# Gate and hid of a feed-forward layer by seven half products in a fixed plan of two slots

## The chip, the cores and the metric

The kernel runs on one core of one Trainium2 chip. The metric is the device time of one launch in microseconds (us). Short names of the engines: PE is TensorE (matmuls), DVE is VectorE, ACT is ScalarE, POOL is GpSimd, SP is the engine that issues most of the DMAs.

## The reference

One transformer block in float32 on `x` of 4 x 1024 x 512 (4 sequences, 1024 tokens, 512 features), with 16 heads of 32 features and a hidden width of 2048. Both norms take a scale and an offset from a condition vector `t`.

```python
def _tc_rmsnorm(x, t, gw, gb, bw, bb):
    g = (t @ gw.T + gb)[:, None, :]
    b = (t @ bw.T + bb)[:, None, :]
    inv_rms = jax.lax.rsqrt(jnp.mean(x * x, axis=-1, keepdims=True) + EPS)
    return g * x * inv_rms + b

def _swiglu(x, gate_w, hid_w, out_w):
    return jax.nn.silu(x @ gate_w.T) * (x @ hid_w.T) @ out_w.T

y = x + _attention(_tc_rmsnorm(x, t, g1w, g1b, b1w, b1b), Wq, Wk, Wv, Wo)
y = y + _swiglu(_tc_rmsnorm(y, t, g2w, g2b, b2w, b2b), gate_w, hid_w, out_w)
out = x + y
```

The change concerns the two products `x @ gate_w.T` and `x @ hid_w.T`.

## The kernel before

Features lie on the 128 partitions in four pieces (`C` = 4), tokens along the free dimension in eight blocks of 512 (`NBLK` = 8, `NB` = 512). The order on PE, DVE, ACT and POOL is the order in which the program is written; SP's DMAs are issued in their order too, each as soon as its buffer is free.

The work runs in *slots*, one turn of the loop `while g < NR + 10`. A slot takes one unit of attention: four heads, 256 queries, two key tiles of 128. Four slots make a group (four heads, 256 queries, all 1024 keys); `kind = g % 4` tells where in the group a slot stands. There are 256 such slots, 32 for each token block. In slot `g` PE computes the scores of unit `g` (`scores`, line 263) into the four PSUM banks of `ps_sc`, and ACT copies them to SBUF (`keep`, 270). DVE keeps a running maximum over the group (`running_max`, 278 and 280, and `fold_max`, 284). In the next slot of kind 0 PE transposes the maxima (`max_T`, mt, 290), DVE reduces them and splits them into three bfloat16 parts (`parts`, 296 to 301), and PE transposes those (`parts_T`, pt, 306), to be copied by ACT (mT, 308). In the slot of kind 1, `spread` (sp, 317) multiplies them out to all partitions and ACT copies the result to `shift` (318). Five slots after its scores a unit is shifted (`shifted`, DVE, 322) and exponentiated (`exponential`, ACT, 327), and a slot later weighted with the values (`weighted`, av, PE, 337). POOL adds the exponentiated tiles of a group with accumulating DMAs (`accumulate`, 351) and folds their two halves with one more (`fold_sum`, 359); `sums` (369) adds over partitions on PE in the slot of kind 3.

Between these pieces stand *chains*: four matmuls of 128 x 128 by 128 x 512 that sum into one bank of the pool `ps` (three banks), and one eviction. Each matmul of a chain is written as four strips of 32 output rows (`mm`, line 102), since `columns` is 32 for most of the loop; the hardware's records show two for each float32 matmul. Chains are key, query and value projections (`project_kq`, `project_v`), the output projection (`project_out`, po), gate and hid (`hidden`, ph: for each token block and each of 16 feature blocks `f`, one chain for gate, one for hid, over four input pieces) and the contraction with `out_w` (`contract`, pc: for four feature blocks together, one chain for each of the four output pieces). They wait in one queue; each slot adds `PACE` = 1.6 to a credit, and each chain taken costs one. Gate is evicted by a tanh on ACT (450) and one DVE operation (452), hid by one DVE operation (454), a contraction by one (466). What is left when attention ends, the feed-forward of the last token block and part of the one before, runs in a tail with nothing beside it.

Weights of a feature block are loaded by `load_f` (512 KB of gate and hid, 256 KB of `out_w`). Norms of the token blocks are put at fixed slots with `between` and `after`.

Of the kernel before, what the change touches and what calls it, by code (L numbers as in the profile page):

```python
# [24 lines left out]
def tile_cond_transformer_block(  # L25
# [7 lines left out]
    vo_w: bass.AP,  # L33
# [19 lines left out]
    PACE = 1.6  # L53
# [6 lines left out]
    ps = ctx.enter_context(tc.tile_pool(name="ps", bufs=3, space=PSUM))  # L60
# [34 lines left out]


    columns = [P]

    def mm(dst, w, moving, start: bool, stop: bool):
        n = columns[0]  # L100
        for k in range(0, P, n):
            nc.tensor.matmul(dst[k : k + n, :], w[:, k : k + n], moving, start=start, stop=stop)  # L102
# [3 lines left out]
    x2, res, h, fw, ow = {}, {}, {}, {}, {}  # L106
    state = {}

    def norm_squares(dst, tag: str, k: int):

        sq = [sb.tile([P, NB], F32, tag="t", name=f"sq{tag}_{2 * k + i}", bufs=3) for i in range(2)]
# [63 lines left out]
    def norm_sum(dst, tag: str):  # L175

        pm = ps.tile([P, NB], F32, tag="w", name=f"pm{tag}")
        for c in range(C):
            sq = sb.tile([P, NB], F32, tag="t", name=f"sq{tag}_{c}", bufs=3)
            nc.scalar.activation(sq, dst[:, c, :], AF.Square)  # L180
            nc.tensor.matmul(pm, ones_mean, sq, start=(c == 0), stop=(c == C - 1))
# [21 lines left out]
    def load_wkq(hg: int):  # L203
        t = sb.tile([P, 2, C, P], F32, tag="fw", name=f"wkq{hg}", bufs=3)
# [4 lines left out]
    def project_kq(b: int, hg: int, which: int, half: int):  # L209
        pp = ps.tile([P, NB], F32, tag="w", name=f"pkq{b}_{hg}_{which}_{half}")  # L210
# [14 lines left out]
    def project_v(b: int, kt: int):  # L225
        half, col = divmod(kt * P, NB)
        pp = ps.tile([P, NB], F32, tag="w", name=f"pv{b}_{kt}")
# [24 lines left out]
    def scores(r: int):  # L252
# [13 lines left out]
        raw[r] = sb.tile([P, HG, 2, HQ], F32, tag="raw", name=f"raw{r}", bufs=RAW)  # L266
        state["sc", r] = sc

    def keep(r: int):
        nc.scalar.copy(raw[r], state.pop(("sc", r)))  # L270

    def running_max(r: int):
        j, u = divmod(r, UN)
        if u == 0:
            return
        if u == 1:
            rmax[j] = sb.tile([P, HG, 2, HQ], F32, tag="rmax", name=f"rmax{j}")
            nc.vector.tensor_tensor(rmax[j], raw[r - 1], raw[r], ALU.max)  # L278
        else:
            nc.vector.tensor_tensor(rmax[j], rmax[j], raw[r], ALU.max)  # L280

    def fold_max(j: int):
        t = rmax[j]
        nc.vector.tensor_tensor(t[:, :, 0, :], t[:, :, 0, :], t[:, :, 1, :], ALU.max)

    def max_T(j: int):
        pt = ps_sc.tile([P, HQ // P, HG, P], F32, tag="sc", name=f"mt{j}")
        for qt in range(HQ // P):
            for i in range(HG):
                nc.tensor.transpose(pt[:, qt, i, :], rmax[j][:, i, 0, qt * P : (qt + 1) * P], ident)  # L290
# [19 lines left out]
    def spread(j: int):  # L310

        shift[j] = sb.tile([P, HG, HQ], F32, tag="shift", name=f"shift{j}")
        t = mT.pop(j)
        for k in range(0, HG, 2):
# [458 lines left out]
```

## Time and profile before

| what | us |
|---|---|
| median of three runs | 2572.88 (2571.51 to 2577.04) |
| the profiled execution | 2572.48 |
| its span | 2570.7 |
| first and last start of a score matmul | 49.3, 2207.0 |
| PE busy in the loop's stretch 565 to 2265 | 1654.21 of 1700 |
| DVE, ACT busy in the same stretch | 1187.01, 941.97 |
| PE busy in the tail, 2265 to 2571 | 298.27 of 306 |

The granted TensorE clock is 0.988 in the mean. Busy time is the union of an engine's instructions; [...]records overlap, and a chain's price is best read from start to start. DMA is the mean busy share of the 16 engines: 0.86 in the stretch of the loop, 0.22 in the tail. 242.24 MB of 475.76 MB go through POOL's queue, which takes 50.8% of the engines' time.

### The profile page before, as it was taken

To read this page: it belongs to the slowest core of one execution; us is meant where nothing else is said; L and a number is where in the kernel's file an instruction comes from. 1 tells how busy PE (TensorE), PEld (TensorE's weight loads), DVE (VectorE), ACT (ScalarE), POOL (GpSimd) and SP (SyncE) were. 2 spreads that over 40 slices of the span, in tenths; PEclk is the share of its full clock that TensorE was granted. 3 is DMA by queue.
4 is the path that set the end of the run, shared out by engine and by line. 5 is a ranking of instruction groups with operands and counts; after the bars stand their busy time and mean duration, and the time that the engine had idled before them with its cause. 6 is when DMAs were issued, how large, how long until landed. Compare 5 with 4: busy or idle time off the path is not lost.

```text
span 2570.7 us, 51245 instructions
## 1 busy us (share of the span) xinstructions
PE 2480.6 (96%) x22520; PEld 1014.6 (39%) x22520; DVE 1595.7 (62%) x1508; ACT 1330.2 (52%) x1229; POOL 256.6 (10%) x271
## 2 busy tenths in 40 slices
PE   8999998999999999999999999999999999999999
PEld 3333333333343443434333343334344434334444
DVE  2666766567777766667777676766777777632221
ACT  3676776565565555555565555555665566410000
POOL 0011111111111111111111111111111111100000
PEclk9999999999999999999999999999999999999999
DMA  5699998898897988888888788888898898922221
GB/s 190 191 250 230 234 232 185 197 229 191 189 200 176 215 194 200 185 214 191 186 193 214 171 194 192 194 204 184 196 205 212 192 207 187 205 77 82 83 82 52
DMA packets 187644, 475.76 MB, mean 185 GB/s; under 512 B 37407, under 2 KB 95767, under 8 KB 159134
## 3 DMA queue, kind: packets, MB, share of 16 engines
q0 software_dynamic: 62448, 242.24, 50.8%
q1 hardware_dynamic: 91392, 219.45, 25.2%
q10 hardware_dynamic: 33582, 10.80, 1.9%
q8 instruction: 177, 2.90, 0.4%
q14 instruction: 45, 0.37, 0.0%
HBM read 196.10 MB, written 34.09 MB: 90 GB/s over the span
## 4 chain that ended last, share of the span: by engine, by line
PE 56%; DMA 9%; DVE 6%; ACT 4%; issue 3%; ACTq 2%; POOL 0%; DVEq 0%; POOLq 0%
PE ph L102 24%; PE pc L102 14%; DMA raw<-raw 7%; PE sc L263 6%; PE av L337 5%; PE po L102 3%; DVE raw L322 3%; ACTq L153 2%; ACT raw L327 2%; PE mt L290 1%; ACT raw L270 1%; PE sum L369 1%; DVE top L296 1%; PE sp L317 1%; DMA res<-x 1%
## 5 line engine op out<-in xcount | busy, mean ns | idle before, releaser
L102 PE MATMUL ph<-x,fw 128*32 128x512 f32 (+1 forms) x6056 | 921.2, 597 | 2.9 <-ACT x L167 2.2
L322 DVE TENSOR_TENSOR raw<-raw,shift 128x2048 f32<-128x2048 f32 x256 | 582.0, 2274 | 109.6 <-ACT shift L318 109.3
L270 ACT COPY raw<-sc 128x2048 f32<-128x2048 f32 x256 | 478.9, 1871 | 306.6 <-PE sc L263 214.4
L327 ACT ACTIVATE raw<-raw 128x2048 f32<-128x2048 f32 x256 | 489.9, 1914 | 129.7 <-DVE raw L322 129.4
L102 PEld LDWEIGHTS ph<-x,fw 128*32 128x32 f32 (+1 forms) x6056 | 309.2, 121 | 501.5 <-issue 472.0
L102 PE MATMUL pc<-h,ow 128*32 128x512 f32 (+1 forms) x3112 | 460.4, 597 | 2.0 <-DVE h L454 2.0
L280 DVE TENSOR_TENSOR rmax<-rmax,raw 128x2048 f32<-128x2048 f32 x128 | 293.0, 2289 | 125.4 <-ACT raw L270 125.3
L351 POOL DMA_DIRECT2D raw<-raw x192 | 169.0, 880 | 1499.0 <-DMA raw<-raw 713.2
L263 PE MATMUL sc<-kq 32*128 32x256 f32 x4096 | 295.1, 402 | 7.5 <-ACT raw L270 7.5
L337 PE MATMUL av<-raw,v 128*32 128x256 f32 x4096 | 279.8, 392 | 14.6 <-ACT avs L363 11.0
L452 DVE SCALAR_TENSOR_TENSOR h<-t,ph 128x512 f32<-128x512 f32 x128 | 88.0, 688 | 299.5 <-ACT t L450 299.5
L263 PEld LDWEIGHTS sc<-kq 32*128 32x128 f32 x4096 | 186.0, 185 | 171.0 <-issue 120.9
L102 PEld LDWEIGHTS pc<-h,ow 128*32 128x32 f32 (+1 forms) x3112 | 152.1, 119 | 254.8 <-issue 235.1
L102 PE MATMUL pkq<-y,wkq 128*32 128x512 f32 (+1 forms) x1784 | 234.8, 599 | 5.9 <-ACT y L167 4.1
L450 ACT ACTIVATE t<-ph 128x512 f32<-128x512 f32 x128 | 76.0, 593 | 313.2 <-PE ph L102 277.4
L466 DVE SCALAR_TENSOR_TENSOR res<-pc,res 128x512 f32<-128x512 f32 x128 | 88.1, 689 | 153.0 <-PE pc L102 152.8
L337 PEld LDWEIGHTS av<-raw,v 128*32 128x32 f32 x4096 | 108.8, 110 | 141.7 <-issue 49.1
L278 DVE TENSOR_TENSOR rmax<-raw,raw 128x2048 f32<-128x2048 f32 x64 | 146.2, 2284 | 24.4 <-ACT raw L270 24.4
L454 DVE TENSOR_TENSOR h<-ph,h 128x512 f32<-128x512 f32 x128 | 87.9, 687 | 86.0 <-PE ph L102 85.8
L308 ACT COPY mT<-pt 12x256 bf16<-12x256 bf16 x64 | 23.1, 360 | 214.5 <-PE pt L306 175.9
L359 POOL DMA_DIRECT2D raw<-raw x64 | 82.9, 1296 | 505.4 <-DMA raw<-raw 462.3
L102 PEld LDWEIGHTS pkq<-y,wkq 128*32 128x32 f32 (+1 forms) x1784 | 72.1, 116 | 136.0 <-issue 121.4
(81 smaller groups left out, 1299.8 us busy)
## 6 DMA issues: line engine op xcount, KB each, us to landing
raw<-raw POOLq DMA_DIRECT2D x192, 1024.0 KB, 8.6
fw<-in_gh_w SPq DMA_DIRECT2D x128, 512.0 KB
ow<-in_out_w SPq DMA_DIRECT2D x128, 256.0 KB
raw<-raw POOLq DMA_DIRECT2D x64, 512.0 KB, 6.4
wkq<-in_kq_w SPq DMA_DIRECT2D x32, 512.0 KB
v<-vs SPq DMA_DIRECT2D x32, 512.0 KB
kq<-kqs SPq DMA_DIRECT2D x31, 512.0 KB
kqs<-st SPq DMA_DIRECT2D x61, 256.0 KB
```

Of the source, the lines that this page charges most:

```text
L102: nc.tensor.matmul(dst[k : k + n, :], w[:, k : k + n], moving, start=start, stop=stop)
L263: nc.tensor.matmul(sc[:, i, k, :], t[rows, kt * P : (kt + 1) * P], t[rows, q0 : q0 + HQ], start=True, stop=True)
L270: nc.scalar.copy(raw[r], state.pop(("sc", r)))
L278: nc.vector.tensor_tensor(rmax[j], raw[r - 1], raw[r], ALU.max)
L280: nc.vector.tensor_tensor(rmax[j], rmax[j], raw[r], ALU.max)
L322: nc.vector.tensor_tensor(t, t, shift[r // UN].unsqueeze(2).to_broadcast([P, HG, 2, HQ]), ALU.add)
L327: nc.scalar.activation(raw[r], raw[r], AF.Exp)
L337: nc.tensor.matmul(av[j][i * DH : (i + 1) * DH, :], v[m][:, kt, i * DH : (i + 1) * DH], raw[r][:, i, k, :], start=(kt == 0), stop=(kt == K ...
L351: nc.gpsimd.dma_start(out=acc[j].rearrange("p h k q -> p (h k q)"), in_=raw[r].rearrange("p h k q -> p (h k q)"), accum_op=ALU.add,)
L452: nc.vector.scalar_tensor_tensor(h[n, f], t, 1.0, pp, ALU.add, ALU.mult)
L454: nc.vector.tensor_tensor(h[n, f], pp, h[n, f], ALU.mult)
L466: nc.vector.scalar_tensor_tensor(r, pp, 0.5, r, ALU.mult, ALU.add)
```

## The change

A feature block's gate and hid are treated as one product of a 2 x 2 block matrix (gate over hid; input pieces 0 and 1, 2 and 3) with a 2 x 2 block of the tokens (the same pieces; 256 tokens left, 256 right), and computed by Strassen's seven products in place of eight. Each product is two matmuls of 128 x 128 by 128 x 256, again in strips of 32 rows.

- `weight_sums` builds four sums of the weights once for each feature block, on DVE, in slots 4 to 51, and stores them in DRAM (`s_w`); `token_sums` builds four differences of the tokens once for each token block, on DVE, one of them in place.
- The products are named 1 to 7. Bank A (`bank_a`, of `ps`) holds gate: product 1 on its left and 5 on its right (`pair_15`). ACT copies product 5 to SBUF (`take_5`), DVE writes left + product 5 to the right (`add_15`), then products 2 and 6 are added by PE onto what stands there (`pair_26`), and product 3 onto the right (`pair_3`). Bank B (`bank_b`, the one bank of `ps_b`) holds hid: ACT copies the right half of A to its right half (`copy_156`) before product 3 comes, PE adds product 7 (`pair_7`), DVE writes right minus product 5 to its left (`sub_5`), and PE adds product 4 (`pair_4`). Then gate and hid are evicted as before (`gate_tanh`, `gate`, `hidden`).
- `ps` has two banks, not three; the third is `ps_b`. Before the token sums exist, `bank` gives every third chain of a projection to `ps_b`.
- From slot `FS` = 60 on, two slots take one feature block, numbered `p` over all token blocks, in a written order: the even slot has `pair_26` and one contraction (`filler`, number `p` - 4; for the first four `p`, a projection kept back for that), the odd slot `pair_7`, `pair_3`, `pair_15` of the next block and `pair_4`. Output projections come in odd slots where they are due. Before that slot the queue runs with `PACE` = 1.5. The tail takes `p` from 104 on.
- `raw` is laid out by key tile first, the running maximum is two DVE operations of 1024 elements a slot (one in the first of a group), and the fold at the end is gone. The fold of the row sums (`fold_sum`) is a DVE operation at the head of the slot of kind 3, not a DMA. `spread` is split in two halves, one ahead of the scores and one behind. The norms of a token block move by a slot here and there.
- `load_f` has two parts, 512 KB and 384 KB; `out_w` and `Wo` are laid out so that each contraction and each output projection loads its own 256 KB.

```diff
-    PACE = 1.6
+    PACE = 1.5
...
-    ps = ctx.enter_context(tc.tile_pool(name="ps", bufs=3, space=PSUM))
+    ps = ctx.enter_context(tc.tile_pool(name="ps", bufs=2, space=PSUM))
+    ps_b = ctx.enter_context(tc.tile_pool(name="ps_b", bufs=1, space=PSUM))
...
+    def bank(name: str):
+
+        turn[0] += 1
+        if "sums" not in state and turn[0] % 3 == 0:
+            return ps_b.tile([P, NB], F32, tag="wb", name=name)
+        return ps.tile([P, NB], F32, tag="w", name=name)
...
-        raw[r] = sb.tile([P, HG, 2, HQ], F32, tag="raw", name=f"raw{r}", bufs=RAW)
+        raw[r] = sb.tile([P, 2, HG, HQ], F32, tag="raw", name=f"raw{r}", bufs=RAW)
...
+    def running_max(r: int, k: int):
         j, u = divmod(r, UN)
+        if u:
+            nc.vector.tensor_tensor(rmax[j], rmax[j], raw[r][:, k, :, :], ALU.max)
+        elif k:
+            rmax[j] = sb.tile([P, HG, HQ], F32, tag="rmax", name=f"rmax{j}")
+            nc.vector.tensor_tensor(rmax[j], raw[r][:, 0, :, :], raw[r][:, 1, :, :], ALU.max)
...
+    def spread(j: int, k: int):
+        if k == 0:
+            shift[j] = sb.tile([P, HG, HQ], F32, tag="shift", name=f"shift{j}")
+        pp = ps.tile([P, 2, HQ], F32, tag="w", name=f"sp{j}_{k}")
+        for i in range(2):
+            nc.tensor.matmul(pp[:, i, :], select[:, k + i, :], mT[j], start=True, stop=True)
+        nc.scalar.copy(shift[j][:, k : k + 2, :], pp)
...
     def fold_sum(j: int):
         t = acc[j]
-        nc.gpsimd.dma_start(out=t[:, :, 0, :], in_=t[:, :, 1, :], accum_op=ALU.add)
+        nc.vector.tensor_tensor(t[:, 0, :, :], t[:, 0, :, :], t[:, 1, :, :], ALU.add)
...
+    def weight_sums(f: int, step: int):
+        if step == 0:
+            state["gh", f] = sb.tile([P, 2, C, P], F32, tag="fw", name=f"gh{f}", bufs=4)
+            nc.sync.dma_start(out=state["gh", f], in_=gh_w[f])
+        else:
+            t = state.pop(("gh", f))
+            a11, a12, a21, a22 = (t[:, i, k : k + 2, :] for i in range(2) for k in (0, 2))
+            o = sb.tile([P, 4, 2, P], F32, tag="fw", name=f"s{f}", bufs=4)
+            nc.vector.tensor_tensor(o[:, 0], a21, a22, ALU.add)
+            nc.vector.tensor_tensor(o[:, 1], o[:, 0], a11, ALU.subtract)
+            nc.vector.tensor_tensor(o[:, 2], a11, a21, ALU.subtract)
+            nc.vector.tensor_tensor(o[:, 3], a12, o[:, 1], ALU.subtract)
+            nc.sync.dma_start(out=s_w[f], in_=o)
...
+    def token_sums(n: int, i: int):
+        b11, b12, b21, b22 = tokens(n)
+        if "sums" not in state:
+            state["sums"] = sb.tile([P, 4, 2, HQ], F32, tag="a", name="sums", bufs=3)
+        t = state["sums"]
+        if i == 0:
+            nc.vector.tensor_tensor(t[:, 0], b12, b11, ALU.subtract)
+        elif i == 1:
+            nc.vector.tensor_tensor(t[:, 1], b22, t[:, 0], ALU.subtract)
+        elif i == 2:
+            nc.vector.tensor_tensor(b12, b22, b12, ALU.subtract)
+        else:
+            nc.vector.tensor_tensor(t[:, 2], b21, t[:, 1], ALU.subtract)
+    def load_f(p: int, part: int):
+        f = p % NF
+        fw[p, part] = sb.tile([P, 4, 2, P], F32, tag="fw", name=f"fw{p}_{part}", bufs=4)
+        if part == 0:
+            nc.sync.dma_start(out=fw[p, 0][:, 0:2], in_=gh_w[f][:, 0].rearrange("p (a c) o -> p a c o", a=2))
+            nc.sync.dma_start(out=fw[p, 0][:, 2:4], in_=s_w[f][:, 0:2])
+        else:
+            nc.sync.dma_start(out=fw[p, 1][:, 0:2], in_=s_w[f][:, 2:4])
+            nc.sync.dma_start(out=fw[p, 1][:, 2], in_=gh_w[f][:, 1, 2:4])
+    def product(dst, w, moving, start: bool = False):
+        for k in range(2):
+            mm(dst, w[:, k, :], moving[:, k, :], start and k == 0, k == 1, True)
+    LEFT, RIGHT = slice(0, HQ), slice(HQ, NB)
+    def pair_15(p: int):
+        b11 = tokens(p // NF)[0]
+        a = bank_a[p] = ps.tile([P, NB], F32, tag="w", name=f"pa{p}")
+        product(a[:, LEFT], fw[p, 0][:, 0], b11, True)
+        product(a[:, RIGHT], fw[p, 0][:, 2], state["sums"][:, 0])
+    def take_5(p: int):
+        fifth[p] = sb.tile([P, HQ], F32, tag="st", name=f"p5_{p}", bufs=2)
+        nc.scalar.copy(fifth[p], bank_a[p][:, RIGHT])
+    def add_15(p: int):
+        a = bank_a[p]
+        nc.vector.tensor_tensor(a[:, RIGHT], a[:, LEFT], fifth[p], ALU.add)
+    def pair_26(p: int):
+        a = bank_a[p]
+        product(a[:, LEFT], fw[p, 0][:, 1], tokens(p // NF)[2])
+        product(a[:, RIGHT], fw[p, 0][:, 3], state["sums"][:, 1])
+    def copy_156(p: int):
+        if "b" not in state:
+            state["b"] = ps_b.tile([P, NB], F32, tag="wb", name="pb")
+            nc.tensor.matmul(
+                state["b"], select[:, 0, :], select.rearrange("p h c -> p (h c)"), start=True, stop=True
+            )
+        bank_b[p] = state["b"]
+        nc.scalar.copy(bank_b[p][:, RIGHT], bank_a[p][:, RIGHT])
+    def pair_7(p: int):
+        product(bank_b[p][:, RIGHT], fw[p, 1][:, 0], tokens(p // NF)[1])
+    def sub_5(p: int):
+        b = bank_b[p]
+        nc.vector.tensor_tensor(b[:, LEFT], b[:, RIGHT], fifth.pop(p), ALU.subtract)
+    def pair_3(p: int):
+        product(bank_a[p][:, RIGHT], fw[p, 1][:, 1], tokens(p // NF)[3])
+    def pair_4(p: int):
+        product(bank_b[p][:, LEFT], fw[p, 1][:, 2], state["sums"][:, 2])
+    def gate_tanh(p: int):
+        state["t", p] = sb.tile([P, NB], F32, tag="t", name=f"t{p}", bufs=2)
+        nc.scalar.activation(state["t", p], bank_a[p], AF.Tanh, scale=0.5)
+    def gate(p: int):
+        h[p] = sb.tile([P, NB], F32, tag="h", name=f"h{p}", bufs=7)
+        nc.vector.scalar_tensor_tensor(h[p], state.pop(("t", p)), 1.0, bank_a.pop(p), ALU.add, ALU.mult)
+    def hidden(p: int):
+        nc.vector.tensor_tensor(h[p], bank_b.pop(p), h[p], ALU.mult)
+    def load_ow(q: int):
+        ow[q] = sb.tile([P, FG, P], F32, tag="ow", name=f"ow{q}", bufs=4)
+        nc.sync.dma_start(out=ow[q], in_=out_w[q // C % (NF // FG), q % C])
+    def contract(q: int, pp, passes):
+        for k in passes:
+            mm(pp, ow[q][:, k, :], h[q // C * FG + k], k == 0, k == FG - 1)
+    def take_contract(q: int, pp):
+        n, d = q // NF, q % C
+        r = res[n][:, d, :]
+        nc.vector.scalar_tensor_tensor(r, pp, 0.5, r, ALU.mult, ALU.add)
+        if q // C % (NF // FG) == NF // FG - 1:
+            nc.sync.dma_start(out=out[n][:, d, :], in_=r)
...
+    FS = BS + 28
+    for f in range(NF):
+        after(3 * f + 4, weight_sums, f, 0)
+        after(3 * f + 6, weight_sums, f, 1)
...
+            for i in range(3):
+                after(g0 + 26, token_sums, n, i)
+            between(g0 + 27, token_sums, n, 3)
...
+            if kind == 1 and m_on:
+                spread(j_m, 0)
             if g < NR:
                 scores(g)
-            if x_on and kind in (2, 3):
+            if kind == 1 and m_on:
+                spread(j_m, 2)
+                mT.pop(j_m)
+            if kind == 3 and s_on:
+                fold_sum(j_s)
...
+                if g == FS - 1:
+                    columns[0] = DH
+                    pair_15(0)
+                    take_5(0)
+                    add_15(0)
...
+            elif even:
+                load_f(p + 1, 1)
+                pair_26(p)
+                copy_156(p)
+                if x_on:
+                    exponential(r_x)
+                if kind == 0 and m_on:
+                    max_T(j_m)
+                    parts(j_m)
+                one, two, evict = filler(p)
+                one()
+                two()
+                if g < NR:
+                    running_max(g, 0)
+                    running_max(g, 1)
+                if evict is not None:
+                    evict()
+                for fn, a in halfway.pop(g, []):
+                    fn(*a)
+            else:
+                load_f(p + 2, 0)
+                if due or len(queue) > FG:
+                    chain(g)()
+                pair_7(p)
+                sub_5(p)
+                pair_3(p)
+                gate_tanh(p)
+                if x_on:
+                    exponential(r_x)
+                pair_15(p + 1)
+                take_5(p + 1)
+                if g < NR:
+                    running_max(g, 0)
+                gate(p)
+                if g < NR:
+                    running_max(g, 1)
+                add_15(p + 1)
+                pair_4(p)
+                hidden(p)
+                if due:
+                    chain(g)()
+                if kind == 3 and s_on:
+                    sums(j_s)
+                    if j_s < direct:
+                        sums_out(j_s)
...
+        p0 = (END - FS) // 2
+        for p in range(p0, NP_):
+            if p + 1 < NP_:
+                load_f(p + 1, 1)
+            pair_26(p)
+            copy_156(p)
+            if p == n * NF - 1:
+                token_sums(n, 0)
+                token_sums(n, 1)
+                token_sums(n, 2)
+            one, two, evict = filler(p, True)
+            one()
+            if p + 2 < NP_:
+                load_f(p + 2, 0)
+            pair_7(p)
+            sub_5(p)
+            pair_3(p)
+            gate_tanh(p)
+            gate(p)
+            if p + 1 < NP_:
+                pair_15(p + 1)
+                take_5(p + 1)
+                add_15(p + 1)
+            pair_4(p)
+            hidden(p)
+            if p == n * NF - 1:
+                token_sums(n, 3)
+            two()
+            evict()
```

## The prediction

> **What bounds the kernel now.** I read the page first, then the chain of waits in order of time over one stretch of the middle, then the timeline of a place where TensorE (PE) stands still, then single rows.
>
> ```profile
> PE 2480.6 (96%) x22520; PEld 1014.6 (39%) x22520; DVE 1595.7 (62%) x1508; ACT 1330.2 (52%) x1229; POOL 256.6 (10%) x271
> L102 PE MATMUL ph<-x,fw 128*32 128x512 f32 (+1 forms) x6056 | 921.2, 597 | 2.9 <-ACT x L167 2.2
> ```
>
> PE is busy 96% of the span, and the largest group, gate and hid (ph), stands idle for only 2.9 us in all: PE sets the time, and what leaves PE leaves the time unless a new wait takes its place. VectorE's (DVE) 62% is a mean: in the attention loop (565 to 2265 us) it is 1187.0 of 1700 us, 70%. The chain over four slots of that loop gives the price of every PE piece from start to start:
>
> ```profile
> 871.15 3.43 PE ph L102 x32
> 874.58 1.02 PE mt L290 x8
> 875.61 3.44 PE pc L102 x8
> 879.04 0.11 PE pt L306 x2
> 879.15 1.08 PE sc L263 x16
> 880.23 0.42 PE sp L317 x4
> 880.65 1.00 PE av L337 x16
> 881.65 3.43 PE pc L102 x32
> ...
> 899.57 0.43 PE sum L369 x8
> ```
>
> Scores (sc) and weighted values (av) cost 2.08 a slot, a chain of 512 columns 3.43, and a block's four extra pieces 1.02 + 0.11 + 0.42 + 0.43 = 1.98. The pieces join without a hole.
>
> ```profile
> 1015.20 0.28 PE L306 MATMUL pt<-ident_bf,split 128*128 128x128 bf16 x2
> 1015.52 0.36 ACT L308 COPY mT<-pt 12x256 bf16<-12x256 bf16 x1 [3.94 <-PE pt L306]
> 1018.17 2.28 DVE L322 TENSOR_TENSOR raw<-raw,shift 128x2048 f32<-128x2048 f32 x1
> 1019.69 1.15 PE L263 MATMUL sc<-kq 32*128 32x256 f32 x16 [1.71 <-ACT raw L270]
> 1020.37 2.28 DVE L278 TENSOR_TENSOR rmax<-raw,raw 128x2048 f32<-128x2048 f32 x1
> 1022.71 1.93 PE L337 MATMUL av<-raw,v 128*32 128x256 f32 x16 [1.87 <-ACT avs L363]
> 1024.41 5.74 PE L102 MATMUL pc<-h,ow 128*32 128x512 f32 x32
> 1030.23 0.69 DVE L466 SCALAR_TENSOR_TENSOR res<-pc,res 128x512 f32<-128x512 f32 x1 [0.78 <-PE pc L102]
> ```
>
> Three things are to be seen here. A tile that PE finishes reaches the next engine 0.05 to 0.1 us after the record's end. DVE operations back to back start 0.08 us before the record ahead ends (2.20 between two of 2.28). And after holes of 1.71 and 1.87 us close together, PE runs at half rate: 1.93 for 1.07, 5.74 for 3.62, so 3.0 us lost; after the first hole alone it still ran the scores at 1.15.
>
> [...]a 512-column chain is 8 groups of four strips, 3.43 / 8 = 0.429; the four 256-column groups of av take 0.88 until the next chain starts (1035.45 to 1036.33), 0.22 each. [...]oT's row has 418 ns.
>
> **The change part by part, against the span of 2570.7.**
>
> *PE work.* Gate and hid cost two chains per feature block, 6.87. Seven half products are 7 x 2 matmuls x 2 records = 28 groups of 256 columns, at 0.429 / 2 = 0.215 to 0.22: 6.0 to 6.2; I take 6.05. Saved: 0.82 x 128 blocks = 105 us (bounds 92 and 107). Contraction, attention and projections keep their matmuls; the one matmul that seeds the second bank is nothing.
>
> *Work beside PE.* Per feature block: two 256-wide copies on ScalarE (ACT), 0.35 each by the avs row, and two 256-wide DVE operations, 0.42. The running maximum becomes seven operations of 1.22 per four slots in place of three of 2.28 and one of 1.22, +0.5. The fold of the row sums leaves the DMA (64 transfers of 512 KB, 6.4 us to landing) for DVE: +1.22 per four slots. Weight sums, 64 operations of about 0.4, lie in the first 52 slots, where DVE has room (64% between 250 and 500 us): nothing. The fourteen weight products need more bytes, 896 KB per block in place of 512, and 16 MB once; the fold's 33 MB go. The DMA share (0.86) stays about where it was, and loads are issued some 20 us ahead: nothing, at worst 10 us.
>
> *Does DVE become the bound?* For four slots of the plan: four shifts 2.2, seven maxima 1.14, six feed-forward operations of 0.61 (gate, hidden and contraction, twice), four of 0.34, one fold 1.14, the parts 2.0, normalize and inverse 0.5: 26.0 us. PE has 4 x 2.08 + 1.98 + 2 x 6.05 + 2 x 3.43 = 29.3. PE stays the bound if the order lets it. Walked through: from the shift in the slot of kind 1 (it waits for the second spread copy, 2.4 us in) to gate in kind 3, DVE works without pause, until 20.3; PE needs 6.8 + 7.2 + 6.4 = 20.4 to reach the row sums, which need the bank that gate frees. It just fits. ACT's 20 us, and 3 of DMA issues, fit easily.
>
> *A new wait.* With one bank given to the second sum, `ps` has two, and one always holds the block being built. At the end of a kind-0 slot the transposed maxima (pt) need the bank of the contraction just finished, so PE waits for the eviction: 0.25 until it starts, 0.69, 0.05: 1.0. Then the spread's first half, which used to stand behind the scores, now comes ahead of them and waits for the mT copy: 0.32 + 0.36 + 0.05 after pt's start, less pt's 0.11: 0.6. Behind it on PE stand the scores and everything else. So 1.6 per four slots, in 50 groups of four: +80 us. Bounds: 1.0 if weight loads and overlaps shorten both (+50), 2.2 if DVE arrives 0.6 late at the eviction (+110).
>
> *Old waits.* PE stood 14.5 us before pt (for DVE) and 17.1 before the row sums (15.8 of it for the fold's DMA). Pt's wait is inside the new one; the sums now wait for DVE. I credit 20 of these 31; between 0 and 31.
>
> *Block edges.* Token sums (four DVE operations of 0.69) stand ahead of the fold and shift at a block's last slot, so pair 4 and the row sums come 1 to 3 us late, seven times, 14; modulation and norms lose as before, and the output projection's PE time (4 x 3.43 a block) lets DVE catch up. +10, bounds 0 and 25. *Clock.* Extra half-rate stretches: +8, bounds 0 and the rival below.
>
> *The ends.* The first 60 slots do the same chains a little later (1.5 for 1.6 a slot). The last 24 blocks of gate and hid, without attention, have a filler of 1.7 between each product and its copy or subtraction, and need no wait: only their share of the 105.
>
> Sum: 2570.7 - 105 + 80 - 20 + 10 + 8 = 2544. The profiled execution took 2572.48, its span and 1.8; the median is 2572.88, so 2 is added: **2546**.
>
> **The rivals.**
> 1. *The holes close up* (pt and the spread pay 1.0, no clock loss, half the edge cost): 2546 - 30 - 8 - 5 = 2503, say 2500 to 2527. For it: PE loads weights ahead in every chain. Against: pt's wait is for an eviction that nothing overlaps.
> 2. *The clock makes it slower.* Place: the end of a kind-0 slot. [...]For it: 1.6 us in every group is close to the holes above. Against: after 1.71 alone the rate stayed full.
> 3. *The fold holds DVE.* DVE's fold at the head of a kind-3 slot needs the third accumulating transfer; the three follow one another, 8.6 to landing each and 0.9 to issue, and by the walk the last lands about 5 us early. The longest took 17.6. If a third of 50 folds come 4 us late, with shift, subtraction and exp behind them on DVE: +66, 2612. For it: PE's old wait for the sums. Against: only 15.8 us of it, with a fourth transfer in the chain.
> 4. *A draw*: DVE a little late everywhere, 0.5 per four slots: 2571.
>
> **How the numbers follow.** Forecast 0.50 (its own range 2527 to 2566), holes closed 0.10, clock 0.20, fold 0.13, draw 0.07. A measurement of this kernel tells 0.2%, 5 us, from no change. Faster is the first two, 0.60; within is the draw, 0.07; slower 0.33. The range runs from 2505, inside the closed holes, to 2612, which leaves the worst clock and fold cases out.
>
> **What would show it.** Right: PE's busy time down by about 100 us; products of 256 columns at 0.215 a group; a hole of 1.0 before pt ended by the contraction's eviction (DVE), and 0.6 before the spread, ended by mT (ACT); slots of 7.8 us in place of 8.4; DVE over 80% in the loop. Wrong: PE waits before pair 2, pair 4 or the row sums of more than 0.5 in the mean (DVE is the bound); half-rate stretches far above the loop's eight or so; DVE idle before the fold, ended by a DMA; fw rows that wait for loads.

## The result, and the profile after

| | before | after |
|---|---|---|
| median of four runs, us | 2572.20 (2561.32 to 2577.04) | 2639.32 (2636.19 to 2641.70) |
| profiled execution's span, us | 2570.7 | 2636.6 |
| start of the scores of slot 60, us | 565.1 | 605.7 |
| from there to the scores of slot 255, us | 1641.1 | 1677.6 |
| the rest, us | 364.5 | 353.2 |
| mean granted clock | 0.988 | 0.977 |

The changed kernel is slower: the ratio is 1.0266, with a 95% interval of 1.0232 to 1.0301. That is 67 us lost where 26 were forecast as gained, outside the range. The work until slot 60 is not quite equal in the two: before had by then run six chains more (four value projections and the first two of gate and hid), after one pair of products (half a chain), so 5.5 x 3.43 = 19 us of PE more in before. So after lost 40.6 + 19 = 60 us in its first 60 slots, and with those 19 us counted, it lost 6 more from slot 60 on: 2030.9 against 2005.6 + 19.

The page of the changed kernel, its engines, the two large DMA queues and two rows:

```profile
PE 2419.9 (92%) x31785; PEld 1154.9 (44%) x31785; DVE 1819.3 (69%) x2116; ACT 1413.9 (54%) x1485; POOL 172.9 (7%) x207
...
q0 software_dynamic: 28656, 208.68, 41.7%
q1 hardware_dynamic: 153840, 286.59, 32.6%
...
L106 PE MATMUL pc<-h,ow 128*32 128x512 f32 x4096 | 467.7, 593 | 0.2 <-DVE rec L392 0.2
L106 PE MATMUL pa<-x,fw 128*32 128x256 f32 x6144 | 381.2, 381 | 8.2 <-DVE pa L501 4.9
```

PE is busy for 61 us less, and its share falls from 96% to 92%: the work went, and standing still came. A clock below 1 hides a part of the saving. (1 - clock) x span is 31 us before and 61 after, so at an equal clock PE would be busy for an estimated 61 + 30 = 91 us less. The products shown have no wait worth the name (8.2 us in 6144 matmuls). The queue of SP (q1) carries 286.59 MB where it had 219.45, POOL's (q0) 208.68 where it had 242.24.

TensorE's waits over the whole execution, in the waits of the changed kernel (engine, tile, line, then what ended the wait, then us in total, times, longest):

```profile
PE sp L325 <- ACT mT L317: 56.5, 64, 6.3
PE pt L315 <- DVE res L554: 39.0, 48, 0.8
...
PE pt L315 <- DVE split L310: 11.9, 6, 2.3
PE pkq L106 <- ACT total L382: 11.7, 5, 3.5
```

The first two are the new wait that was forecast. The second of them is as forecast: 0.81 each from the end of a record, and about 1.0 with the chain priced at 3.43 from start to start. The first is longer than forecast, 0.88 in the mean and up to 6.3. Where the 6.3 and its like come from shows in the timeline of the changed kernel, in the second group of a token block (start, duration, engine; in brackets the idle time before and what ended it; ACTq is the DMA issue on ACT's instruction stream):

```profile
945.26 1.87 ACT L285 COPY raw<-sc 128x2048 f32<-128x2048 f32 x1 [0.70 <-PE sc L278]
945.40 10.11 ACTq L168 DMA_DIRECT2D rec<-invss  x4
...
945.62 0.33 SPq L406 DMA_DIRECT2D res<-in_x  x1
...
952.58 0.69 DVE L554 SCALAR_TENSOR_TENSOR res<-pc,res 128x512 f32<-128x512 f32 x1 [0.41 <-PE pc L106]
953.33 0.27 PE L315 MATMUL pt<-ident_bf,split 128*128 128x128 bf16 x2 [0.81 <-DVE res L554]
...
955.61 0.36 ACT L516 COPY pb<-pa 128x256 f32<-128x256 f32 x1 [8.48 <-DMA rec<-invss]
955.88 1.91 ACT L335 ACTIVATE raw<-raw 128x2048 f32<-128x2048 f32 x1
957.69 0.34 ACT L317 COPY mT<-pt 12x256 bf16<-12x256 bf16 x1
...
958.09 0.36 PE L325 MATMUL sp<-mT,select 12*128 12x256 bf16 x1 [4.49 <-ACT mT L317]
...
960.73 1.93 PE L345 MATMUL av<-raw,v 128*32 128x256 f32 x16
```

Four DMA issues of the row sums' inverse (`sums_in`, L168) occupy ACT's stream for 10.11 us. Behind them in program order stand `copy_156` (L516), the exponential and the mT copy (L317), so ACT is idle for 8.48 us, mT is 4.0 us late, and so are PE's spread and its scores. The two copies and the exponential that ACT must then make up are 0.36, 1.91 and 0.34. Then PE runs at half rate: 1.93 for an av that takes 1.07 (granted clock 0.50 from 957.5 to 964.2). The issue starts at about the time when the block's 1 MB of `res` (L406) and weight loads are put on SP's queue.

What the issue waits for is in the trace, too. Most of the 10.11 us lie ahead of the last of the four issues, which starts only at 955.20. At the same place of the next block, the view puts ACT's idle time down to the load of `res` by name:

```profile
1233.29 0.31 ACTq L168 DMA_DIRECT2D rec<-invss  x1
1233.69 0.36 ACT L516 COPY pb<-pa 128x256 f32<-128x256 f32 x1 [8.92 <-DMA res<-in_x]
```

The instruction records name the reason. The load of `res` at 945.62 and the fourth issue name the same semaphore (number 100), and the fourth issue has a wait for it: the load's 16 signals to it came between 954.20 and 955.18, the issue started at 955.20. At five of the eight loads of `res` one of the four issues waits in this way for the load whose semaphore it shares, for 5.9 to 8.8 us, 38.1 us in all, and starts 0.02 us behind the load's last signal each time; the four together then hold ACT for 8.6 to 11.6 us, against 3.9 in the median. In before no issue of `rec` waits for `res`, and none waits longer than 2.9 us.

The first 60 slots, in windows of before (window: length, busy time of PE, PEld, DVE, ACT, POOL with the number of instructions, clock, DMA share, GB/s):

```profile
150.00:250.00 100.00, 97.69 (x1020) 38.88 (x1019) 69.95 (x54) 73.22 (x76) 11.66 (x12) 1.00 0.97 240
250.00:350.00 100.00, 97.87 (x1006) 39.98 (x1002) 67.21 (x56) 70.93 (x75) 11.69 (x12) 1.00 0.94 226
450.00:550.00 100.00, 93.49 (x922) 37.67 (x926) 59.66 (x55) 62.22 (x65) 10.40 (x11) 0.96 0.87 213
```

and in the same windows of after:

```profile
150.00:250.00 100.00, 90.17 (x845) 36.09 (x841) 63.48 (x71) 57.83 (x63) 6.03 (x7) 0.94 0.85 220
250.00:350.00 100.00, 85.50 (x836) 33.04 (x828) 70.52 (x72) 63.61 (x63) 6.90 (x8) 0.95 0.83 226
450.00:550.00 100.00, 85.51 (x798) 33.09 (x791) 68.22 (x76) 59.90 (x61) 7.78 (x9) 0.93 0.88 223
```

Before Strassen's products even start, PE runs 13 to 17% fewer matmuls per 100 us, at a clock of 0.93 to 0.95 where it was 0.96 to 1.00. What it waits for shows in the timeline of after at one such place:

```profile
116.08 2.49 DVE L179 TENSOR_TENSOR y<-y,inva 128x512 f32<-128x512 f32 x4
...
118.49 1.22 DVE L305 TENSOR_REDUCE top<-mt 128x8 f32<-128x1024 f32 x1
...
120.61 0.28 PE L315 MATMUL pt<-ident_bf,split 128*128 128x128 bf16 x2 [2.32 <-DVE split L310]
...
121.71 0.60 ACT L235 ACTIVATE st<-pkq 128x512 f32<-128x512 f32 x1 [7.27 <-DMA kqs<-st]
...
122.20 0.34 ACT L317 COPY mT<-pt 12x256 bf16<-12x256 bf16 x1
...
122.60 0.37 PE L325 MATMUL sp<-mT,select 12*128 12x256 bf16 x1 [1.70 <-ACT mT L317]
```

Two things come together. DVE scales a norm (L179, 2.49 us) just ahead of the maxima (L305), so pt is 2.32 late. And ACT's eviction of a projection (L235) waits 7.27 us for an earlier store of its own kind to leave the buffer; the mT copy stands behind it.

### The profile page after: what moved, and what is told of

It reads as the page before. It is cut to its first block, busy times and chain, and to the rows that moved or that the text cites. A ratio compares the mean times of both kernels' runs of the same rounds, so it can differ in the third digit from the quotient of the medians.

```text
span 2636.6 us, 71583 instructions
## 1 busy us (share of the span) xinstructions
PE 2419.9 (92%) x31785; PEld 1154.9 (44%) x31785; DVE 1819.3 (69%) x2116; ACT 1413.9 (54%) x1485; POOL 172.9 (7%) x207
## 3 DMA queue, kind: packets, MB, share of 16 engines
q0 software_dynamic: 28656, 208.68, 41.7%
q1 hardware_dynamic: 153840, 286.59, 32.6%
## 5 line engine op out<-in xcount | busy, mean ns | idle before, releaser
L335 ACT ACTIVATE raw<-raw 128x2048 f32<-128x2048 f32 x256 | 489.9, 1913 | 58.8 <-DVE raw L330 38.1
L290 DVE TENSOR_TENSOR rmax<-rmax,raw 128x1024 f32<-128x1024 f32 x384 | 469.0, 1221 | 59.8 <-ACT raw L285 56.5
L106 PE MATMUL pc<-h,ow 128*32 128x512 f32 x4096 | 467.7, 593 | 0.2 <-DVE rec L392 0.2
L106 PE MATMUL pa<-x,fw 128*32 128x256 f32 x6144 | 381.2, 381 | 8.2 <-DVE pa L501 4.9
L359 POOL DMA_DIRECT2D raw<-raw x192 | 165.7, 863 | 2063.1 <-ACT raw L335 1000.9
L345 PE MATMUL av<-raw,v 128*32 128x256 f32 x4096 | 286.2, 398 | 11.3 <-ACT raw L335 11.2
L106 PE MATMUL pa<-sums,fw 128*32 128x256 f32 x4096 | 269.1, 380 | 0.0
L106 PEld LDWEIGHTS pa<-x,fw 128*32 128x32 f32 x6144 | 200.0, 111 | 155.2 <-issue 12.6
L106 PE MATMUL pkq<-y,wkq 128*32 128x512 f32 (+1 forms) x1760 | 241.7, 616 | 21.0 <-ACT total L382 11.7
L106 PEld LDWEIGHTS pc<-h,ow 128*32 128x32 f32 x4096 | 128.0, 110 | 243.5 <-issue 217.3
L516 ACT COPY pb<-pa 128x256 f32<-128x256 f32 x128 | 46.0, 360 | 295.2 <-PE pa L106 133.9
L106 PEld LDWEIGHTS pa<-sums,fw 128*32 128x32 f32 x4096 | 133.4, 110 | 88.7 <-issue 1.0
L106 PE MATMUL pb<-sums,fw 128*32 128x256 f32 x2048 | 134.9, 381 | 12.0 <-DVE pb L523 12.0
L293 DVE TENSOR_TENSOR rmax<-raw 128x1024 f32<-128x1024 f32 x64 | 78.1, 1220 | 96.3 <-PE mt L299 54.5
```

The lines of the kernel that those rows point to most:

```text
L290: nc.vector.tensor_tensor(rmax[j], rmax[j], raw[r][:, k, :, :], ALU.max)
L293: nc.vector.tensor_tensor(rmax[j], raw[r][:, 0, :, :], raw[r][:, 1, :, :], ALU.max)
L335: nc.scalar.activation(raw[r], raw[r], AF.Exp)
L345: nc.tensor.matmul(av[j][i * DH : (i + 1) * DH, :], v[m][:, kt, i * DH : (i + 1) * DH], raw[r][:, k, i, :], start=(kt == 0), stop=(kt == K ...
L359: nc.gpsimd.dma_start(out=acc[j].rearrange("p k h q -> p (k h q)"), in_=raw[r].rearrange("p k h q -> p (k h q)"), accum_op=ALU.add,)
L516: nc.scalar.copy(bank_b[p][:, RIGHT], bank_a[p][:, RIGHT])
```

## The experiments

Three places were in question: the wait at pt and the spread (with the clock behind it, which the second rival made the main loss), ACT's stream held by the row sums' issue, and the first 60 slots. Each run's ratio is against before on the same chip, with a 95% interval. A saving of a run is its ratio's difference from 1.0266, times 2572; the intervals make it uncertain by some 10 us. Starts of slot 60, and lengths of stretches, are of single executions: e1 and e7, which have the same program up to there, start slot 60 at 600.6 and 608.6, so these carry some 8 us of chance.

**e1: pt in a bank of the scores.**

```diff
-        pt = ps.tile([P, HQ // P, P], BF16, tag="w", name=f"pt{j}")
+        pt = ps_sc.tile([P, HQ // P, P], BF16, tag="sc", name=f"pt{j}")
```

> Against the changed kernel's 2639 us. Theory of the joint: at the end of every kind-0 slot PE waits about 0.98 us before pt because pt needs the bank that the contraction's eviction frees (48 times, 46.9 us in the loop). With pt in the scores' banks, which are free there, those holes go: 40 to 50 us less, and the wait before the spread (for the mT copy) stays as it is, about 0.7 us a time. Rival, that another engine is as late as the bank (the parts on DVE, or ACT in front of the mT copy): the hole before pt goes but the one before the spread grows by as much, less than 15 us gained.

Measured: 2606.81, ratio 1.0159 (1.0133 to 1.0185), 28 us saved. The waits of e1:

```profile
PE sp L325 <- ACT mT L317: 50.9, 28, 7.2
PE sp L325 <- DVE res L554: 21.5, 36, 0.6
```

Pt's wait for the contraction is gone, but the spread behind it now waits for the same eviction, 36 times, since its own bank is also the one that the contraction holds. A bank for pt alone is half a cure, and the saving stays below the 40 us expected.

**e2: the old pace in the first 60 slots.**

```diff
-    PACE = 1.5
+    PACE = 1.6
-            if s > BS + 15:
+            if s > BS + 14:
```

> Against 2639 us. Credit of 1.6 a slot in the first 60 slots in place of 1.5, as before the change; nothing else. Theory of the beat: at 1.5, twelve chains take exactly eight slots, so five of the six norms of the inputs put their scaling on a kind-0 slot ahead of the parts (pt 2.1 us late, five times) and their roots ahead of the row sums' copy (chains after the row sums 2.5 us late); at 1.6 they spread over the kinds. 25 to 45 us less, and the first 60 slots' PE idle of 87 us falls towards the 35 of the kernel before. Rivals, that the weight sums or the lost third bank cause the loss there: within 10 us of 2639.

Measured: 2610.74, ratio 1.0171 (1.0148 to 1.0194), 24 us saved. Slot 60 starts at 584.1, 21.6 earlier, with the same chains done; from 50 us to there PE stands still for 52.1 us, where it was 65.8 in after and 27.1 in before (the union of PE's records; the 87 and 35 of the expectation are too high); from there to slot 255 it is 1673.8, about as in after. Between 50 and 600 us the waits of e2 have

```profile
PE pt L315 <- DVE split L310: 5.7, 2, 3.3
...
PE pkq L106 <- ACT total L382: 0.5, 1, 0.5
```

for 11.9 and 11.7 in after. Pt gains little by that, since two new waits for ACT's evictions, 5.8 us, stand ahead of it; ACT's waits for its own stores (`st <- kqs`) fall from 36.5 to 19.3. A reading of the written order: at 1.5 a slot, the twelve key, query and value chains of a norm take exactly eight slots, so the norms' work falls at slots 8, 16, 24, 32 and 40, always a slot of kind 0, whose maxima it delays; at 1.6 the beat drifts. That the pace matters is shown. That it is the beat, and not the number of chains a slot, is argued: no run parts the two.

**e3: the row sums' issue moved to the end of its slot, behind pt** (still on ACT's stream).

```diff
-            if kind == 0 and o_on:
-                sums_in(j_o)
...
                 parts_T(j_m)
+            if kind == 0 and o_on:
+                sums_in(j_o)
```

> Against 2639 us. The four DMA issues that bring the inverted row sums back (sums_in, on ACT's queue) are put at the end of the kind-0 slot, behind the mT copy, in place of ahead of the second sum's copy and exp. Theory of ACT's queue: where their transfer is late, ACT stands behind them (8.5 us once a block), and with it the mT copy, the spread and the shift: slots 4 and 5 of a block fall from about 23.5 to 17, six times, 40 to 50 us less. Rival, that these slots are late for the large load of the residual and would wait for it elsewhere: under 15 us.

Measured: 2798.40, ratio 1.0891 (1.0863 to 1.0920), clock 0.946: 161 us lost, where 40 to 50 were expected as gained. The waits of e3:

```profile
PE sp L325 <- ACT shift L326: 112.7, 58, 5.0
...
PE sp L325 <- ACT mT L317: 31.7, 64, 3.4
```

The wait for mT falls from 56.5 to 31.7, which is what the move was for. But the issue now stands behind the mT copy and ahead of the shift copies, so the spread's second half waits 1.9 for the first half's copy in nearly every group. That adds a second hole close behind the first. From slot 60 to 255 the lost clock (1 - clock, summed over the time) grows from 23.9 to 97.3 us. The loss that the second rival feared is real, then, but a group's 1.7 us of waits in the changed kernel (0.81 + 0.88) did not bring it in general, with eight stretches at half rate from slot 60 to 255, and about twice as much here (0.8 + 0.5 + 1.9) did.

**e5: the row sums' issue on SP's queue in place of ACT's, at the same place in the program.**

```diff
-    def spread_inverse(tag: str, t, rows: int, n: int):
+    def spread_inverse(tag: str, t, rows: int, n: int, by=nc.scalar):
...
-            nc.scalar.dma_start(
+            by.dma_start(
...
-        spread_inverse(f"s{j}", t, DH, HQ)
+        spread_inverse(f"s{j}", t, DH, HQ, nc.sync)
```

> Against 2639 us. The four issues that bring back the inverted row sums stand where they stood, but on SP's queue in place of ACT's. Theory of ACT's queue (an issue whose transfer waits for another one to land holds every copy behind it, and e3 only moved that wait from one copy to a worse one): slots 4 and 5 of a block fall from 23.5 to about 17, the spread's hole from 1.14 to about 0.7, some of the first 60 slots too: 45 to 75 us less. Rival, that SP's queue then holds the weight loads as long and PE waits for fw: less than 20, or slower, with PE waits ended by fw's DMA.

Measured: 2601.47, ratio 1.0131 (1.0106 to 1.0156), 35 us saved, below the 45 to 75 expected but above the rival's 20. The waits of e5:

```profile
PE pt L315 <- DVE res L554: 39.0, 48, 0.8
PE sp L325 <- ACT mT L317: 32.7, 64, 3.4
```

The spread's wait is 32.7 / 64 = 0.51 each, close to the forecast's walk where ACT is on time (0.32 + 0.36 + 0.05 after pt's start, less its record of 0.27: 0.46). From slot 60 to 255 it takes 1645.6, 32.0 less than after; the lost clock there is 6.8 for 23.9. In after, the two slots at offsets 4 and 5 of a block took 15.1 and 9.2 us in the median; here they take 10.1 and 6.7, as elsewhere. At the place of the timeline above, the four issues of `rec` took 3.40 us on SP's queue (from 943.10 on), where they had held ACT for 10.11. Whether a different semaphore for the fourth issue, on ACT, would do the same was not tried.

**e6: the whole spread behind the scores**, as before the change: `spread(0)` behind `scores`, then `weighted`, then `spread(2)`.

> Against 2639 us. The spread's two halves come behind the scores, as before the change, with the weighted values between them; pt keeps its bank. Theory of the joint: the mT copy (0.7 us after pt) is covered by the scores, so the holes between pt and the spread go, 1.14 x 49 = 56 us in the loop and 10 in the first 60 slots; the shift starts about 2 us later, which DVE can take in. 35 to 65 less. Rival, that DVE then reaches the row sums' bank too late (by the walk it just fits): the holes come back before the row sums and pair 4, less than 15.

Measured: 2645.22, ratio 1.0292 (1.0260 to 1.0323): no gain, where 35 to 65 us were expected. Most of PE's wait at the spread went (11.2 us for mT are left), and others came: the wait of mt for ACT's copy of the scores rose from 1.6 to 17.9 us. That the shift on DVE needs the spread early is the likely reason; no run shows it apart.

**e7: e1, and pt placed ahead of the contraction's last input piece**, in the feed-forward slots of kind 0.

```diff
-            half = FG // 2
+            half = FG // 2 if tail else FG - 1
...
                 one()
+                if kind == 0 and m_on:
+                    parts_T(j_m)
                 two()
```

> Against 2639 us. Pt has a bank of the scores and stands ahead of the last quarter of the contraction, in place of behind it; nothing else. Theory of the joint: pt's hole (46.9 us) and most of the spread's (55.7, of which the part with late ACT stays, some 25) go together, with the half-rate stretches that they cause: 70 to 100 less, twice or three times e1, where the second hole grew. Rival, that DVE's parts are not ready there: a hole of 0.5 or more before pt, less than 50.

Measured: 2622.81, ratio 1.0208 (1.0178 to 1.0237), 15 us saved; from slot 60 to 255 it takes 1658.3, 19.3 less than after. With ACT's stream still held, the spread goes on waiting for mT (42.9 us) in this run, and where mT is on time, for the contraction's eviction (31.0). e7 contains e1's edit and saves no more than it (15 for 28 us), far from the 70 to 100 expected: the earlier place alone gained nothing. Whether e1's place would serve as well beside e2 and e5 was not run.

**e4, e8, e11: the weight sums.** e4 leaves them out whole: `load_f` reads the same number of bytes from the plain weights. e8 is e4 with e2's pace. e11 leaves out only DVE's four operations for each feature block and keeps the load and the store, with one buffer fewer in use. The edits of e4 and of e11:

```diff
-    for f in range(NF):
-        after(3 * f + 4, weight_sums, f, 0)
-        after(3 * f + 6, weight_sums, f, 1)
...
```

```diff
-            a11, a12, a21, a22 = (t[:, i, k : k + 2, :] for i in range(2) for k in (0, 2))
-            o = sb.tile([P, 4, 2, P], F32, tag="fw", name=f"s{f}", bufs=4)
-            nc.vector.tensor_tensor(o[:, 0], a21, a22, ALU.add)
...
+            o = t.rearrange("p i (a c) o -> p (i a) c o", a=2)
```

> Leaves out the weight sums (their loads, DVE operations and stores in slots 4 to 51); the products read plain weights of the same sizes in their place. Against 2639 us. Theory of the weight sums (DMA at its limit and DVE ahead of the shift in the first 60 slots): most of the 65 us lost there come back, 40 to 65 less. Theory of the beat: 5 to 15 less.

> e2 and e4 together (credit of 1.6; the weight sums left out, plain weights of the same sizes read in their place). Against 2639 us, where e2 alone gave 29 and e4 alone 38. If the beat of the norms and the weight sums are two causes of the loss in the first 60 slots: 55 to 70 less, with slot 60 at about 550 us (605.7 in the changed kernel, 565.1 before). If they are one cause, the weight sums being late only where the norms fall on kind 0, or the reverse: 40 to 48 less.

> Leaves out the DVE operations of the weight sums alone (64 operations of 0.42 us); loads and stores of the same sizes stay, with one tile of the weight pool less in use. Against 2639 us, where leaving out all of it gave 38. If DVE ahead of the shift is what the weight sums cost: 25 to 40 less. If their transfers are (17 MB where the DMA queues are fullest): under 12.

Measured: e4 2601.17, ratio 1.0134 (1.0110 to 1.0157), 34 us saved, slot 60 at 574.7. e8 2591.12, ratio 1.0069 (1.0044 to 1.0094), 51 us saved, slot 60 at 566.1. e11 2629.03, ratio 1.0229 (1.0194 to 1.0263), 10 us, slot 60 at 600.7; its interval overlaps that of after. So the sums cost 34 us; DVE's operations account for 10 of them, give or take 10, and the transfers for most of the rest. Between 50 and 600 us the waits of e4 have

```profile
ACT st L235 <- DMA kqs<-st: 7.8, 2, 5.4
...
PE pkq L106 <- ACT total L382: 5.3, 5, 1.2
```

for 36.5 (9 times) and 11.7 in after: with the sums' traffic gone from SP's queue (269.81 MB for 286.59), ACT waits less for the projections' own stores. That this is the way in which the transfers cost time is not shown: in e5 the same wait of ACT came to 61.8 us (13 times) between 50 and 600 us, and slot 60 still started at 600.8, no later than in after. Pace and sums together give 51 where their single savings add to 58: within the intervals they add up, but 51 lies between what was expected of one cause (40 to 48) and of two (55 to 70), so the run does not decide it.

**e9: e2, e5 and e7 together.** **e10: e9 with e6.**

> Against 2639 us and against before. e2's credit of 1.6, e5's row sums on SP and e7's pt inside the contraction, together. If the three causes are separate, their gains add: 29 + 45 to 75 + 70 to 100 less some 20 that e5 and e7 share in the spread's hole, 2455 to 2515, below the kernel before. If they share one cause (ACT's queue), the sum is little better than the best of them: 2530 or more.

> e9 and the spread behind the scores (e6) together. Against e9's 2565 us: in e9 the hole stands before the spread (0.98 us, 47 times, ended by the contraction's eviction on DVE), for the spread's own bank. Theory that the one free bank of two is the joint: behind the scores that wait is covered, 46 us of holes go, and 25 to 45 us with them, 2520 to 2540, below the kernel before. Rival, that DVE then sets the pace (in e6 slots of kinds 1 and 2 grew by 0.4 and 0.3): 2555 or more.

Measured: e9 2565.37, ratio 0.9979 (0.9961 to 0.9997), 74 us saved; the three single savings, 24 + 35 + 15, make 74. So exact a match is chance: the profiled executions put 13 us before slot 60 (592.7), where e2 alone had 21.6, and 52 between there and slot 255. The timeline of e9 at the end of an even slot:

```profile
992.37 2.78 PE L106 MATMUL pc<-h,ow 128*32 128x512 f32 x24
995.08 0.29 PE L315 MATMUL pt<-ident_bf,split 128*128 128x128 bf16 x2
995.30 1.06 PE L106 MATMUL pc<-h,ow 128*32 128x512 f32 x8
995.40 0.36 ACT L317 COPY mT<-pt 12x256 bf16<-12x256 bf16 x1 [1.74 <-PE pt L315]
996.43 0.69 DVE L554 SCALAR_TENSOR_TENSOR res<-pc,res 128x512 f32<-128x512 f32 x1 [0.77 <-PE pc L106]
...
997.18 0.28 PE L325 MATMUL sp<-mT,select 12*128 12x256 bf16 x1 [0.81 <-DVE res L554]
```

Pt is inside the contraction and mT is copied under it, so one wait of 0.81 is left, for the eviction that frees the spread's bank. e10 moves the spread behind the scores to take that one away too, and is slower: 2605.11, ratio 1.0126 (1.0089 to 1.0164). The waits of e10:

```profile
PE mt L299 <- ACT raw L285: 21.3, 27, 2.8
PE av L345 <- ACT raw L335: 20.3, 19, 2.4
PE sc L278 <- ACT raw L285: 17.6, 9, 2.9
```

Other places now wait for the scores' copy and the exponential. The loss is not everywhere: in the median a regular group takes 30.6 us here for 31.0 in e9, while the slots at offsets 5, 6, 17 and 19 of a block take 2.1, 2.3, 1.1 and 1.1 us more, and the lost clock from slot 60 to 255 is 20.5 for 5.1. A likely reason is that DVE can't make up for a later spread there; it is argued, not shown. In e9 DVE is busy for 322 of 400 us between 1000 and 1400, ACT for 243:

```profile
1000.00:1400.00 400.00, 380.44 (x5454) 187.39 (x5446) 322.11 (x373) 243.18 (x247) 31.87 (x37) 1.00 0.84 204
```

e9 is the fastest version found, and at most some 0.4% faster than before: little more than the bound of what can be told.

## Why the prediction was wrong

*PE work, -105: right.* A product of pa in the timeline of after starts at 946.01 and the next at 946.87; a product is four 256-column groups, so 0.215 a group, as taken. Busy time fell by an estimated 91 at an equal clock, just under the lower bound of 92. In e9 a mean slot takes 1625.6 / 195 = 8.34 us; before it took 1641.1 / 195 = 8.42, after 8.60.

*A new wait, +80: the size right without ACT's delay, and wrong with it.* Pt cost what was taken for it. The spread, taken at 0.6, has 0.51 by the record's end in e5, but 0.88 in after. So the bank as the new limit was foreseen rightly, in place and size, by an argument and not by luck. A regular group of four slots in after takes 10.0 + 6.7 + 7.2 + 6.9 = 30.8 us, and the forecast's walk has 29.3 + 1.6 = 30.9.

*"ACT's 20 us, and 3 of DMA issues, fit easily": failed.* This is one of the two steps that failed. It added durations of ACT and did not ask how long an issue can hold the stream. Issues of `rec<-invss` held it for up to 11.6 us, with `copy_156`, the exponential and the mT copy behind it, and PE behind mT. e5 shows the price: 35 us. The spread's waits fell by 56.5 - 32.7 = 24 us, the lost clock from slot 60 to 255 by 23.9 - 6.8 = 17. The issue stood on ACT before, too, but there it never waited for the load of `res`; in after it did at five block edges, 38.1 us in all, and the spread's first half now stood ahead of the scores, so that PE felt it. With e5 the time from slot 60 on is 1997.2 us, 27 less than the 2005.6 + 19 of before: what the forecast had for the whole kernel, 26. That these agree so well is partly luck, since several smaller terms below were off both ways.

*"The first 60 slots do the same chains a little later", at nothing: failed.* This is the other step, and the larger. Those 60 slots lost 60 us. PE stood still for 65.8 us between 50 us and slot 60, against 27.1 before, and lost 29.0 us to the clock, against 10.2. The pace costs 24 us by e2, and the weight sums 34 by e4; both together 51 by e8. The sum had priced DVE's 64 operations ("DVE has room") and the 16 MB ("nothing, at worst 10 us") apart from each other and each against a mean share. DVE's part was indeed small (10 us or less by e11). The transfers were not, against the "nothing, at worst 10 us"; how they cost PE its time stays open. In before the DMA engines were busy for 0.94 to 0.97 of the time between 150 and 350 us; in after it is 0.83 to 0.85, so the share alone does not explain it.

With e8's 51 and e5's 35, 86 of the 93 us between forecast and result are accounted for, if the two add, which no run tests. The first 60 slots are not fully explained by it: in e8 slot 60 starts at 566.1, where before started it at 565.1 with 19 us more done, so some 20 of the 60 us stay open. The spread's new place is not it, since e6, which puts it back, starts slot 60 later still, at 615.6. The third bank given away is a rival there that no run tried apart.

*Old waits, -20, and block edges, +10: both too hopeful.* The row sums' waits fell from 17.1 to 11.5 us only; pt's wait for DVE is gone behind slot 60, but grew to 11.9 ahead of it. At the edges pair 4 waited 12.0 us for the subtraction (8 times) and the second norm's sums (pmf) 11.4 for the contraction's eviction (6 times), waits that before does not have; these 23 lie inside the bounds of 0 to 25.

*The clock, +8: low.* (1 - clock) x span grew by 30 us, 19 of it before slot 60. In e5 and e9 it shrank together with the holes, so it is counted in their savings. The second rival had the right sign, and its loss shows in e3, but not its place: from slot 60 to 255 after has eight stretches at half rate, 3.41 to 10.24 us long, which cost the 23.9, and a clock of 1.0 between them, so that regular groups with their 0.8 and 0.5 to 0.9 us of waits mostly ran at the full rate. Its odds of 0.20 rested on an estimate of the author's; how much standing still is enough was not shown.

*Does DVE become the bound? "It just fits": right, as far as seen.* DVE is busy for 308 of 400 us in after's loop, 77% where over 80 was forecast (the forecast's list of a group's DVE work adds to 25.4 us, not 26.0), PE's waits for pair 2, pair 4 and the row sums are small (12.0, eight times, is the largest), and e6 and e10 gained nothing by a later spread. The third rival fell: DVE waited for an accumulating transfer before the fold once, 7.1 us. *The tail* got 11 us shorter (364.5 to 353.2 from slot 255 on), where 24 x 0.82 = 20 were its share; after has three contractions more to do there (35 for 32), 10 us.

## What to carry to other kernels

A stage that the change doesn't speak of still has to be walked through when its pace, banks or queues change: here the first 60 slots lost nearly as much as the whole kernel did. ACT's instruction stream was held here for as long as its DMA issues took, their own wait for another transfer included (four issues, up to 11.6 us), so what stands behind it in program order, and who waits for that, belongs in the sum; moving the issue to SP's queue (e5) gave back 35 us for a few words of code. And when a bank is given away, follow all who use the pool: pt's new bank only passed the wait on to the spread, and in e9 39.2 us of it are still there.

## What the runs showed of the hardware

- Waits of 0.8 and 0.5 us in every group of four slots left the clock nearly whole (1.00 from 1000 to 2200 us of e5); with a further hole of 1.9 us close behind in nearly every group (e3), the mean clock of the whole run fell to 0.946, and some 150 of 2796 us were lost to it. Of after's eight stretches at half rate from slot 60 to 255, six followed a hole of 3.7 to 6.3 us in one piece; the one at 650.2 followed holes of 1.23 and 0.45 us, the one at 1104.2 holes of 0.81 and 1.19. In before, the ones at 643.0 and 813.6 followed single holes of 1.35 and 1.42, shorter than the 1.71 after which the forecast saw the scores at the full rate: the length of one hole does not tell, by these traces, whether the clock falls.
- DMA issues held their engine's stream while they waited for another transfer. Four issues held ACT for 3.9 us in the median in after, and for 8.6 to 11.6 at the five places where one of them shared a semaphore with a load of 1 MB and started 0.02 us behind its last signal. Single issues took 309 to 2478 ns, the wait ahead of them not counted (after, 900 to 1200), and 318 to 2240 ns on SP (e5, the same window).
- In after, PE adds products onto what DVE and ACT wrote into a PSUM bank. The four rows of the products (14336 matmuls) show 0.0, 1.2, 8.2 and 12.0 us of waiting in all, of which 1.2, 4.9 and 12.0 were for the copy or the operation that writes the bank, and their matmuls took 380 to 389 ns in the mean, where av's of the same 256 columns took 392 in before. The forecast took this adding as free; no trace of before shows it.
